# Graph layers on one Trainium2 core: the first group's loads moved ahead of the weights, bias rows made from broadcast loads

## Chip, cores and metric

The kernel runs on one core of a Trainium2 chip. The metric is the device time of one execution in microseconds. The engines are named as in the profile: PE is TensorE (PEld its weight loads), DVE is VectorE, ACT is ScalarE, POOL is GpSimd, SP is SyncE, whose queue issues every DMA of this kernel.

## What is computed

There are 128 graphs of 128 nodes with 64 features, and a dense adjacency matrix of each, with zeros. Two layers follow one another, each with a residual sum and a normalisation:

```python
x = layernorm(x + L0(x, adj));  x = layernorm(x + L1(x, adj))

def L0(x, adj, W1, b1, W2, b2):            # 64 -> 192 -> 64
    mask = adj > 0;  W1a, W1b = W1[:64], W1[64:]
    h = relu((x @ W1a)[:, :, None, :] + (x[:, :, None, :] - x[:, None, :, :]) @ W1b + b1)
    hm = einsum('bjkh,bjk->bjh', h, mask)
    return hm @ W2 + mask.sum(-1)[..., None] * b2

def L1(h, A, W1, b1, W2, b2, W_ih, b_ih, W_hh, b_hh):
    m = relu(relu(h @ W1 + b1) @ W2 + b2)
    msg = relu(A @ m)
    i_r, i_z, i_n = split(msg @ W_ih.T + b_ih);  h_r, h_z, h_n = split(h @ W_hh.T + b_hh)
    r, z = sigmoid(i_r + h_r), sigmoid(i_z + h_z)
    return (1 - z) * tanh(i_n + r * h_n) + z * h
```

## The kernel before

The 128 graphs are worked in 32 groups of four (`G`). The hard part is layer 0's sum over neighbours of a relu of a sum. The kernel writes `h` as a node's part plus a neighbour's part, gathers the neighbours' parts and sums absolute values. For each group:

- `load`: SP issues four transfers, `adjT` (256 KB), `xT` in two halves, `x`.
- `masks` (POOL) makes `maskT` from `adjT`; `ranks` (PE `pc`, then VectorE `rankT`) numbers each node's neighbours; `degrees` and `counts` (`nseg`, `wseg`, `npad`) and `offsets` (`side`, `past`, `own`, `own32`) say which overflow rows belong to which node; `turned` and `places` lead to `place`.
- `picks` makes one-hot selection matrices from `rankT` (`pick0`) and `place` (`pick1`).
- `values0` and `values1`: PE multiplies `xT` with `wall`, the joined weights of layer 0, and adds a bias with `call3`; ScalarE copies the result to `uv`.
- `pieces` splits a part of `uv` into three bf16 numbers `b0`, `b1`, `b2` that add up to it: a ScalarE cast, a VectorE subtraction, a ScalarE cast, a POOL subtraction.
- `seed` (ScalarE writes the node's part to PSUM), `gather` (twelve PE matmuls of `pick` and `b`, line 592, add the neighbours' parts) and `reduce` (VectorE sums absolute values, line 608) come 24 times per group. This is the main loop.
- `together` and `sums` collect the results, `second` to `update` finish layer 0 and compute layer 1 (`gw1`, `gw2`, `gb1`, `gb2`, `wm`, `wx`, `bias3`).

The order on each engine is written out by hand. `TIMETABLE` gives each part a list of times; a part is a Python generator, and each time runs it up to its next `yield`. Group g is shifted by 768 (`PER`). All steps of all groups are sorted by time and recorded in that order, so each engine's instructions, SP's DMAs too, stand in the order of the timetable. An engine does not overtake a waiting instruction. Group 1's `load` is due before much of group 0's work, and group 1's `masks`, `ranks` and `degrees` are recorded ahead of group 0's first gather.

Everything of the setup is recorded ahead of the plan, lines 95 to 225: constants (`ident`, `upper`, `incl`, `strict`, `iota`), weights, and bias rows. PE adds a bias by a matmul of ones with a bf16 matrix that holds, in rows 0 to 2 (and again 64 to 66), three bf16 pieces of the bias that add up to it. The helper `three_rows` makes it from one row: on one partition it casts and subtracts, and each piece goes to its rows by DMA, as many as halves and repetitions ask (6 for `call3`, 12 for `gb2`, 12 for `bias3`). `wall` is computed on 64 partitions and copied to the other 64 by a DMA (line 192). PSUM tiles of the small products come from a pool `ps_w` with two buffers, so a product waits for the reading of the last but one.

The path at the end of the kernel (a loop over graphs behind a flag, for graphs with too many neighbours) has the same helpers.

Of the kernel before, what the change touches and what calls it, by code (L numbers as in the profile page):

```python
# [8 lines left out]
F32 = mybir.dt.float32  # L9
BF16 = mybir.dt.bfloat16  # L10
I32 = mybir.dt.int32
AF = mybir.ActivationFunctionType
ALU = mybir.AluOpType
AX = mybir.AxisListType

N = 128
F = 64
H = 192
HC = 96
G = 4  # L20
K = 64
V = H + F
W0 = 8
W1 = 4
# [25 lines left out]


# [17 lines left out]
def adj_resnorm_kernel(  # L69
# [19 lines left out]
    nc = tc.nc  # L89
# [6 lines left out]
    make_identity(nc, ident)  # L96
    ident_h = const.tile([N, N], BF16, name="ident_h")
    nc.vector.tensor_copy(ident_h, ident)
    upper = const.tile([N, N], F32, name="upper")
    make_upper_triangular(nc, upper)  # L100

    incl = const.tile([N, N], BF16, name="incl")
    nc.vector.tensor_copy(incl, upper)
    incl2 = const.tile([N, N], BF16, name="incl2")
    nc.vector.tensor_copy(incl2, upper)
    nc.vector.memset(incl2[0:K, K:N], 0.0)

    halves = const.tile([N, 2], BF16, name="halves")
    nc.vector.memset(halves, 0.0)
    for h in range(2):  # L110
        nc.vector.memset(halves[h * K : (h + 1) * K, h : h + 1], 1.0)
    strict = const.tile([N, N], BF16, name="strict")
    nc.vector.tensor_sub(strict, upper, ident)
    strict_w = const.tile([N, N], BF16, name="strict_w")
    nc.vector.tensor_scalar_mul(strict_w, strict, -float(W1))
    ones_h = const.tile([N, N], BF16, name="ones_h")
    nc.vector.memset(ones_h, 1.0)
    ones = const.tile([1, N], F32, name="ones")
    nc.vector.memset(ones, 1.0)
    nhalf = const.tile([N, G], F32, name="nhalf")  # L120
    nc.gpsimd.memset(nhalf, -0.5)
    nseg_all = const.tile([N, NB], BF16, name="nseg_all")

    wb = const.tile([F, H], F32, name="wb")
    nc.sync.dma_start(wb, w1[F : 2 * F, :])
    wa = const.tile([F, H], F32, name="wa")
    nc.sync.dma_start(wa, w1[0:F, :])
    iota = const.tile([N, N], BF16, name="iota")

    wall = const.tile([N, 4 * N], F32, name="wall")  # L130
    nc.vector.tensor_add(wall[0:F, 0:H], wa, wb)
    nc.vector.tensor_scalar_mul(wall[0:F, V : V + H], wb, -1.0)
    w2c = const.tile([HC, 2, F], F32, name="w2c")
    for c in range(2):
        nc.sync.dma_start(w2c[:, c, :], w2[c * HC : (c + 1) * HC, :])
    nc.vector.tensor_scalar_mul(w2c, w2c, 0.5)

    def row(name, src, n):
        t = const.tile([1, n], F32, name=name)
        nc.sync.dma_start(t, src.rearrange("(o n) -> o n", o=1))  # L140
        return t

    def three_rows(name, src, n, times, halves=2):

        t = const.tile([N, times, n], BF16, name=name)
        nc.vector.memset(t, 0.0)
        rest = src
        for c in range(3):
            piece = const.tile([1, n], BF16, name=f"{name}_piece{c}")
            nc.vector.tensor_copy(piece, rest)  # L150
            for at in (c, F + c)[:halves]:
                for i in range(times):
                    nc.sync.dma_start(t[at : at + 1, i, :], piece)
            if c < 2:
                left = const.tile([1, n], F32, name=f"{name}_left{c}")
                nc.vector.tensor_sub(left, rest, piece)
                rest = left
        return t


    call = const.tile([1, V], F32, name="call")
    nc.sync.dma_start(call[:, 0:H], b1.rearrange("(o h) -> o h", o=1))
    b2row = row("b2row", b2, F)
    b2bc = const.tile([N, F], F32, name="b2bc")
    wT = const.tile([HC, 4, F], F32, name="wT")
    b1c = const.tile([HC, 2], F32, name="b1c")
    for c in range(2):
        nc.sync.dma_start(b1c[:, c : c + 1], b1[c * HC : (c + 1) * HC].rearrange("(h o) -> h o", o=1))
    with tc.tile_pool(name="ps_c", bufs=1, space=bass.MemoryType.PSUM) as ps_c:
        ips = ps_c.tile([N, N], F32, name="ips")  # L170
        nc.tensor.matmul(ips, ones_h, strict, start=True, stop=True)
        nc.vector.tensor_copy(iota, ips)
        b2ps = ps_c.tile([N, F], F32, name="b2ps")
        nc.tensor.matmul(b2ps, ones, b2row, start=True, stop=True)
        nc.vector.tensor_copy(b2bc, b2ps)

        tps = ps_c.tile([HC, 4, F], F32, name="tps")
        for c in range(4):
            at = (V, V + HC, 0, HC)[c]
            nc.tensor.transpose(tps[:, c, :], wall[0:F, at : at + HC], ident[0:F, 0:F])  # L180
        nc.vector.tensor_copy(wT, tps)
        dps = ps_c.tile([F, 2, F], F32, name="dps")
        for d in range(2):
            for c in range(2):
                nc.tensor.matmul(dps[:, d, :], wT[:, 2 * d + c, :], w2c[:, c, :], start=c == 0, stop=c == 1)
        nc.vector.tensor_copy(wall[0:F, H:V], dps[:, 0, :])
        nc.vector.tensor_copy(wall[0:F, V + H : 4 * N], dps[:, 1, :])
        cps = ps_c.tile([1, F], F32, name="cps")
        for c in range(2):
            nc.tensor.matmul(cps, b1c[:, c : c + 1], w2c[:, c, :], start=c == 0, stop=c == 1)  # L190
        nc.vector.tensor_add(call[:, H:V], cps, b2row)
    nc.sync.dma_start(wall[F:N, :], wall[0:F, :])
    call3 = three_rows("call3", call, V, 1)

    def twice(name, src):
        t = const.tile([N, N], F32, name=name)
        nc.vector.memset(t, 0.0)
        for h in range(2):  # L200
            nc.sync.dma_start(t[h * F : (h + 1) * F, h * F : (h + 1) * F], src)
        return t

    gw1 = twice("gw1", g_w1)
    gw2 = twice("gw2", g_w2)
    gb1 = const.tile([N, 1], F32, name="gb1")
    for h in range(2):
        nc.sync.dma_start(gb1[h * F : (h + 1) * F], g_b1.rearrange("(h o) -> h o", o=1))
    gb2 = three_rows("gb2", row("gb2row", g_b2, F), F, G, 1)


    wm = const.tile([N, H], F32, name="wm")
    wx = const.tile([N, H], F32, name="wx")
    for h in range(2):
        hs = slice(h * F, (h + 1) * F)
        nc.sync.dma_start(wm[hs, 0:F], w_ihT[:, 128:H])
        nc.sync.dma_start(wm[hs, F:H], w_ihT[:, 0:128])
        nc.sync.dma_start(wx[hs, :], w_hhT)
    bi = row("bi", b_ih, H)
    bh = row("bh", b_hh, H)  # L220
    bcat = const.tile([1, 256], F32, name="bcat")
    nc.vector.tensor_copy(bcat[:, 0:F], bi[:, 128:H])
    nc.vector.tensor_add(bcat[:, F:H], bi[:, 0:128], bh[:, 0:128])
    nc.vector.tensor_copy(bcat[:, H:256], bh[:, 128:H])
    bias3 = three_rows("bias3", bcat, 256, 2)
# [13 lines left out]
    def tail_parts(s, work, ps_w, n, store):  # L239


        name = s["name"]
# [47 lines left out]
        def message2():  # L290
            p = ps_w.tile([N, n, F], F32, tag="w", name=f"pn{name}")
            nc.tensor.matmul(p, ones_h, gb2, start=True, stop=False)
            for i in range(2):
                nc.tensor.matmul(p[:, 2 * i : 2 * i + 2, :], s["m1"][:, i, :], gw2, start=False, stop=i == 1)
            yield
            s["m2"] = work.tile([N, n, F], F32, tag="m2", name=f"m2_{name}")
            nc.scalar.activation(s["m2"], p, AF.Relu)
# [13 lines left out]
        def gates():  # L311
# [3 lines left out]
            for h in range(2):  # L315
                nc.tensor.matmul(ps[h], ones_h[hs[h]], bias3[hs[h]], start=True, stop=False)
# [42 lines left out]
    with ExitStack() as fast:  # L359
# [6 lines left out]


        zeros = loads.tile([N, 512], BF16, name="zeros", bufs=1)
        nc.vector.memset(zeros, 0.0)
        for i in range(3):  # L370
            p = ps_g.tile([N, 2, 512], F32, tag="g", name="pv")
            for c in range(2):
                nc.tensor.matmul(p[:, c, :], ones_h, zeros, start=True, stop=True)
# [13 lines left out]
        def prep_parts(s):  # L387
            g = s["g"]
# [116 lines left out]
            def values(i):  # L505
                def part():
# [4 lines left out]
                    for h in range(2):  # L511
                        ks = slice(h * F, (h + 1) * F)
                        nc.tensor.matmul(ps[h][:, 0:V], ones_h[ks], call3[ks, 0, :], start=False, stop=True)  # L513
# [8 lines left out]
            def pieces():  # L522

                v = s["uv"][:, :, H : V + H]

                def piece(c):
                    s[f"b{c}"] = prep.tile([N, G, H + F], BF16, tag=f"b{c}", name=f"b{c}_{g}")
                    return s[f"b{c}"]

                nc.scalar.copy(piece(0), v)  # L530
                yield
                r = prep.tile([N, G, H + F], F32, tag="r", name=f"r{g}", bufs=1)
                nc.vector.tensor_sub(r, v, s["b0"])  # L533
                yield
                nc.scalar.copy(piece(1), r)  # L535
                yield
                nc.gpsimd.tensor_tensor(piece(2), r, s["b1"], ALU.subtract)  # L537
# [146 lines left out]
        plan = {}  # L684
        for g in range(ng):
# [7 lines left out]
            for name, times in TIMETABLE.items():  # L693
                run = parts[name]()
                for t in times:
                    plan.setdefault(g * PER + t, []).append(run)
# [127 lines left out]
```

## Time and profile before

| | us |
|---|---|
| median of 3 runs (lowest, highest) | 1123.66 (1123.61, 1123.87) |
| time of the profiled execution | 1123.7 |
| its span | 1121.9 |
| VectorE busy | 1046.6 |
| PE busy | 989.1 |
| ScalarE busy | 929.2 |
| POOL busy | 790.0 |
| group 0's `adjT` issued | 25.48 |
| first reduction of line 608 | 50.23 |

The span runs from the first to the last instruction of the profile; busy times are sums of instruction times, and instructions of one engine may overlap a little. In the profile's lines `a<-b` says that `a` is made from `b`. The bracket at the end of a timeline line is the idle time of the engine before it and what released it. SPq is SP's queue, with the time it takes to issue a DMA.

### The profile page before, as it was taken

Reading aid. Unit: us, or ns where it says so; the run is one execution under the profiler, and the core shown is the slowest. Engines: PE = TensorE matmul, PEld = TensorE weight load, DVE = VectorE, ACT = ScalarE, POOL = GpSimd, SP = SyncE. Lnnn points to the kernel's source line nnn. Section 1 sums busy time; section 2 is a strip of 40 time slices with the busy share of each in tenths; the row PEclk is TensorE's granted clock in tenths of the full one; section 3 lists DMA queues with packets and bytes.
Section 4 is the critical chain, followed back from the end, with each engine's and each line's share of the span. In section 5 each row is a group of like instructions: output and inputs, shape, how many; then the busy total and the mean of one; then the engine's idle time right before and its main releaser. Section 6 shows DMA issues by size and latency. Waiting matters only on the chain.

```text
span 1121.9 us, 33471 instructions
## 1 busy us (share of the span) xinstructions
PE 989.1 (88%) x13434; PEld 767.5 (68%) x13434; DVE 1046.6 (93%) x2446; ACT 929.2 (83%) x1570; POOL 790.0 (70%) x1161
## 2 busy tenths in 40 slices
PE   2689999999999999999999999999999999999872
PEld 1457777777777777777777776777777677777761
DVE  3599999999999999999999999999999999999961
ACT  0489988988888898888989888898888889888850
POOL 0365667777867877787777778777777877787656
PEclk9999999999999999999999999999999999999985
DMA  1200000000000000000000000000000000000000
GB/s 32 64 1 21 21 21 10 13 25 25 25 26 25 14 14 25 26 25 25 26 20 7 25 25 26 25 26 25 2 25 25 26 25 25 26 7 2 7 6 26
DMA packets 21722, 23.73 MB, mean 21 GB/s; under 512 B 4727, under 2 KB 17402, under 8 KB 21562
## 3 DMA queue, kind: packets, MB, share of 16 engines
q1 hardware_dynamic: 21562, 21.54, 6.4%
q8 instruction: 107, 1.75, 0.6%
q14 instruction: 53, 0.43, 0.1%
HBM read 17.19 MB, written 4.19 MB: 19 GB/s over the span
## 4 chain that ended last, share of the span: by engine, by line
DVE 46%; PE 29%; ACT 15%; issue 5%; POOL 3%; SPq 1%; DMA 0%; DVEq 0%; ACTq 0%; POOLq 0%
DVE part L608 29%; PE pv L592 11%; ACT pv L561 10%; PE pw L267 6%; DVE pick L500 4%; PE pu L510 4%; PE ph L650 3%; ACT uv L517 3%; DVE r L533 3%; PE ph L649 2%; DVE rankT L401 2%; DVE n L331 2%; DVE stats L248 1%; DVE own L450 1%; DVE rh L330 1%
## 5 line engine op out<-in xcount | busy, mean ns | idle before, releaser
L608 DVE TENSOR_REDUCE part<-pv 128x192 f32<-128x768 f32 x768 | 697.3, 944 | 10.8 <-PE pv L592 7.0
L592 PE MATMUL pv<-b,pick 64*128 64x192 bf16 x9216 | 509.9, 244 | 55.6 <-ACT pv L561 49.3
L592 PEld LDWEIGHTS <-pick 64*128 64x128 bf16 x9216 | 379.7, 94 | 166.2 <-issue 135.4
L561 ACT COPY pv<-uv 128x768 f32<-128x768 f32 x512 | 404.1, 807 | 30.8 <-DVE part L608 30.4
L630 POOL TENSOR_TENSOR part<-part 128x384 f32<-128x384 f32 x128 | 132.6, 1036 | 235.7 <-DVE part L608 235.5
L561 ACT COPY pv<-us 128x768 f32<-128x768 f32 x256 | 206.7, 808 | 28.9 <-DVE part L608 23.7
L650 PE MATMUL ph<-ownT,part 128*96 128x128 f32 x512 | 95.6, 282 | 23.0 <-POOL part L637 22.9
L650 PEld LDWEIGHTS ph<-ownT,part 128*96 128x96 f32 x512 | 70.4, 167 | 35.5 <-POOL part L637 35.5
L517 ACT COPY uv<-pu 128x512 f32<-128x512 f32 x128 | 68.5, 586 | 23.4 <-PE pu L513 21.2
L500 DVE TENSOR_SCALAR pick<-rankT 128x512 bf16<-128x512 bf16 x256 | 86.5, 349 | 0.0
L510 PE MATMUL pu<-wall,xT 64*128 64x512 f32 x256 | 82.0, 645 | 0.0
L267 PE MATMUL pw<-w2c,hmT 96*128 96x64 f32 x512 | 79.9, 289 | 0.0
L632 POOL TENSOR_TENSOR part<-part 128x192 f32<-128x192 f32 x128 | 75.9, 593 | 5.2
L634 POOL TENSOR_TENSOR part<-part 128x192 f32<-128x192 f32 x128 | 74.3, 591 | 5.0
L637 POOL TENSOR_TENSOR part<-part 128x192 f32<-128x192 f32 x128 | 75.1, 597 | 1.4 <-DVE part L608 1.4
L649 PE MATMUL ph<-ident,part 128*96 128x128 f32 x256 | 73.1, 286 | 2.7 <-POOL part L634 1.8
L267 PEld LDWEIGHTS pw<-w2c,hmT 96*128 96x128 f32 x512 | 68.7, 195 | 9.8 <-issue 5.0
L255 POOL TENSOR_TENSOR rs<-ve,nhalf 128x4 f32<-128x4 f32 x64 | 67.0, 1047 | 5.3
L537 POOL TENSOR_TENSOR b<-r,b 128x1024 bf16<-128x1024 f32 x32 | 68.2, 2130 | 0.5 <-ACT b L535 0.5
L392 POOL TENSOR_SCALAR maskT<-adjT 128x512 bf16<-128x512 f32 x32 | 49.7, 1554 | 26.6 <-DMA adjT<-in_adjT_dram 26.6
L656 ACT COPY hmT<-ph 96x512 f32<-96x512 f32 x64 | 36.6, 572 | 33.5 <-PE ph L650 33.5
L572 PE MATMUL pz<-uv,own 128*128 128x192 f32 x256 | 62.5, 368 | 0.9 <-ACT uv L517 0.5
(150 smaller groups left out, 1638.5 us busy)
## 6 DMA issues: line engine op xcount, KB each, us to landing
adjT<-in_adjT_dram SPq DMA_DIRECT2D x32, 256.0 KB, 2.7
xT<-in_xT_dram SPq DMA_DIRECT2D x64, 64.0 KB, 2.5
x<-in_x_dram SPq DMA_DIRECT2D x32, 128.0 KB, 2.3
out_dram<-o SPq DMA_DIRECT2D x32, 128.0 KB, 2.0
gb<-gb_piece SPq DMA_DIRECT2D x12, 0.1 KB, 1.6
bias<-bias_piece SPq DMA_DIRECT2D x12, 0.5 KB, 1.7
wall<-wall SPq DMA_DIRECT2D x1, 128.0 KB
call<-call_piece SPq DMA_DIRECT2D x6, 0.5 KB, 1.7
```

The source lines that it names most:

```text
L267: nc.tensor.matmul(p[:, i, :], s["hmT"][:, i, c, :], w2c[:, c, :], start=c == 0, stop=False)
L500: nc.vector.tensor_scalar(s[name][:, i], s[src], float(first + i), None, ALU.is_equal)
L510: nc.tensor.matmul(ps[h], s["xT"][ks, i, :], wall[ks, :], start=True, stop=False)
L517: nc.scalar.copy(uv[:, 2 * h + i, :], ps[h])
L561: nc.scalar.copy(v, src.rearrange("p (c b h) -> p c b h", c=1, b=1).to_broadcast(list(v.shape)))
L592: nc.tensor.matmul(v[:, h, j, :], pick[ks, a + j, i, :], s[f"b{c}"][ks, i, F : F + H], start=False, stop=c == 2, skip_group_check=True,)
L608: nc.vector.tensor_reduce(into, view(s["pv", i, k]).rearrange("p c b h -> p h c b"), AX.XY, ALU.add, apply_absolute_value=True,)
L630: nc.gpsimd.tensor_tensor(f[:, 0:2], f[:, 0:2], f[:, 2:4], ALU.add)
L632: nc.gpsimd.tensor_tensor(f[:, 0], f[:, 0], f[:, 1], ALU.add)
L637: nc.gpsimd.tensor_tensor(f[:, 0], f[:, 0], f[:, 1], ALU.add)
L649: nc.tensor.transpose(p[:, i, c, :], s["part", i0 + i][:, 0, cs], ident)
L650: nc.tensor.matmul(p[:, i, c, :], s["part1", i0 + i][:, 0, cs], s["ownT"][:, i0 + i, :], start=False, stop=True, skip_group_check=True,)
```

## The change

The setup becomes a generator that the plan runs at five times (`SETUP`), and group 0 has its own times (`FIRST`), so both are recorded together in one order:

- Group 0's `load` (-5000) comes first of all on SP. Then the setup's first step issues `wab` (both halves of layer 0's first weights on each half of the partitions, two transfers), `w2c`, `b1c`, and five biases. Each bias is loaded to all 128 partitions by a source that repeats the row. The other weights (`gw1`, `gw2`, `gb1`, `wm`, `wx`) are the setup's last step, at -3000: after all of group 0's preparation in the record, and ahead of group 1's `load` (-752). `gw1` and `gw2` are cleared by VectorE in that step, ahead of their transfers.
- The bias matrix is computed on all partitions for all 576 columns at once: three casts, two subtractions, and a product or multiply-add of each piece with a column of `at`, which is one in the rows where that piece belongs. It needs no DMA. The matmuls that repeat a bias read it with a repeating pattern (`each`). `gb2` now has its rows twice, and is halved before.
- `wall` is computed on all 128 partitions, so its copy is gone; `wT` is written twice over for that.
- Constants are recorded in the order of their use; the small products share `ps_w`.
- For group 0 `pieces` runs graph by graph, four passes over 256 columns; the other groups have one pass over 1024 columns as before.

```diff
+SETUP = (-4990, -4988, -4987, -4981, -3000)
+FIRST = {
+    "load": (-5000,), "masks": (-4989,), "ranks": (-4986, -4985), "degrees": (-4984, -4983), "counts": (-4982,),
+    "offsets": (-4980, -4979, -4966, -4965, -4964, -4963, -4962, -4962), "turned": (-4978, -4977),
+    "values0": (-4976, -4975, -4974), "values1": (-4971, -4970, -4969), "pieces": (-4972, -4968, -4959, -4958),
+    "places": (-4961, -4960), "pick0": (-4973, -4973, -4967, -4967, -4957, -4957, -4956, -4956),
 }
...
-    def three_rows(name, src, n, times, halves=2):
...
-    nc.sync.dma_start(wall[F:N, :], wall[0:F, :])
-    call3 = three_rows("call3", call, V, 1)
...
-    gb2 = three_rows("gb2", row("gb2row", g_b2, F), F, G, 1)
...
-    bias3 = three_rows("bias3", bcat, 256, 2)
...
+    call3, bias3, gb2 = three[:, 0:V], three[:, V : V + 256], three[:, V + 256 : NBI]
...
+    def each(t, n):
+        return t.rearrange("p (o c) -> p o c", o=1).to_broadcast([t.shape[0], n, t.shape[1]])
+
+    def setup(ps_g, ps_w):
+        def spread(t, src):
+            nc.sync.dma_start(t, src.rearrange("(o n) -> o n", o=1).to_broadcast(list(t.shape)))
+        for h in range(2):
+            nc.sync.dma_start(wab[h * F : (h + 1) * F], w1.rearrange("(c f) h -> f c h", c=2))
+        nc.sync.dma_start(w2c, w2.rearrange("(c h) f -> h c f", c=2))
+        nc.sync.dma_start(b1c, b1.rearrange("(c h) -> h c", c=2))
+        spread(b2bc, b2)
+        spread(bias[:, 0:H], b1)
+        spread(bi, b_ih)
+        spread(bias[:, V + F : V + 256], b_hh)
+        spread(bias[:, V + 256 : NBI], g_b2)
...
+        yield
+        nc.vector.tensor_copy(iota, ips)
+        nc.vector.tensor_add(wall[:, 0:H], wab[:, 0, :], wab[:, 1, :])
+        nc.vector.tensor_scalar_mul(wall[:, V : V + H], wab[:, 1, :], -1.0)
...
+        yield
...
+        nc.vector.tensor_copy(wT, tps.rearrange("p c (o f) -> p c o f", o=1).to_broadcast([HC, 4, 2, F]))
+        yield
...
+        nc.vector.tensor_copy(wall[:, H:V], dps[:, 0, :])
+        nc.vector.tensor_copy(wall[:, V + H : 4 * N], dps[:, 1, :])
+        nc.vector.tensor_add(bias[:, H:V], cps, b2bc)
...
+        nc.vector.tensor_add(at, ident[:, 0:3], ident[:, F : F + 3])
+        piece = const.tile([N, NBI], BF16, name="piece")
+        for c in range(3):
+            nc.vector.tensor_copy(piece, bias)
+            if c == 0:
+                nc.vector.tensor_scalar(three, piece, at[:, c : c + 1], None, ALU.mult)
+            else:
+                nc.vector.scalar_tensor_tensor(
+                    out=three, in0=piece, scalar=at[:, c : c + 1], in1=three, op0=ALU.mult, op1=ALU.add
+                )
+            if c < 2:
+                nc.vector.tensor_sub(bias, bias, piece)
+        yield
+        for t, src in ((gw1, g_w1), (gw2, g_w2)):
+            nc.vector.memset(t, 0.0)
+            for h in range(2):
+                nc.sync.dma_start(t[h * F : (h + 1) * F, h * F : (h + 1) * F], src)
+        for h in range(2):
+            hs = slice(h * F, (h + 1) * F)
+            nc.sync.dma_start(gb1[hs], g_b1.rearrange("(h o) -> h o", o=1))
+            nc.sync.dma_start(wm[hs, 0:F], w_ihT[:, 128:H])
+            nc.sync.dma_start(wm[hs, F:H], w_ihT[:, 0:128])
+            nc.sync.dma_start(wx[hs, :], w_hhT)
...
-            nc.tensor.matmul(p, ones_h, gb2, start=True, stop=False)
+            nc.tensor.matmul(p, ones_h, each(gb2, n), start=True, stop=False)
...
+                for gs in [slice(i, i + 1) for i in range(G)] if g == 0 else [slice(0, G)]:
+                    v = s["uv"][:, gs, H : V + H]
+                    nc.scalar.copy(b[0][:, gs], v)
...
+                    nc.vector.tensor_tensor(r[:, gs], v, b[0][:, gs], ALU.subtract)
...
+                    nc.scalar.copy(b[1][:, gs], r[:, gs])
...
+                    nc.gpsimd.tensor_tensor(b[2][:, gs], r[:, gs], b[1][:, gs], ALU.subtract)
+                    yield
...
+        name, g, run = "setup", -1, setup(ps_g, ps_w)
+        for t in SETUP:
+            plan.setdefault(t, []).append(run)
...
-                for t in times:
+                for t in FIRST.get(name, times) if g == 0 else times:
```

## Prediction

> **What bounds the kernel now.** I read the page first, then the windows over the start, then the timeline and the chain of waits there. The page gives the whole: VectorE 93% busy, and its largest group, the reduction on line 608, waits 10.8 us in 1122.
>
> ```profile
> PE 989.1 (88%) x13434; PEld 767.5 (68%) x13434; DVE 1046.6 (93%) x2446; ACT 929.2 (83%) x1570; POOL 790.0 (70%) x1161
> L608 DVE TENSOR_REDUCE part<-pv 128x192 f32<-128x768 f32 x768 | 697.3, 944 | 10.8 <-PE pv L592 7.0
> ```
>
> So from the first reduction on VectorE is the bound, and time can come only from the start or from less VectorE work later. The windows show where the start ends (columns: length, then busy us of PE, PEld, DVE, ACT, POOL):
>
> ```profile
> 0.00:20.00 20.00, 6.11 (x25) 3.08 (x26) 7.00 (x36) 1.28 (x1) 1.12 (x9) 1.00 0.10 18
> 20.00:40.00 20.00, 7.54 (x31) 4.06 (x31) 8.82 (x33) 2.41 (x5) 4.50 (x8) 1.00 0.28 77
> 40.00:60.00 20.00, 13.90 (x118) 9.46 (x117) 11.29 (x27) 12.38 (x21) 7.14 (x11) 0.91 0.13 39
> 60.00:80.00 20.00, 15.64 (x233) 11.33 (x228) 19.43 (x30) 16.84 (x26) 11.17 (x16) 1.00 0.01 2
> ```
>
> VectorE is idle for over half of the first 60 us. The timeline of that stretch (start, length, instruction, idle before and releaser) says why:
>
> ```profile
> 4.64 2.39 SPq L201 DMA_DIRECT2D gw<-in_g_w_dram  x4
> 7.08 1.23 SPq L208 DMA_DIRECT2D gb<-in_g_b_dram  x2
> 13.99 7.49 SPq L153 DMA_DIRECT2D gb<-gb_piece  x12
> 22.15 0.59 SPq L218 DMA_DIRECT2D wx<-in_w_hhT_dram  x1
> 25.48 0.36 SPq L379 DMA_DIRECT2D adjT<-in_adjT_dram  x1
> 28.32 1.50 POOL L392 TENSOR_SCALAR maskT<-adjT 128x512 bf16<-128x512 f32 x1 [26.61 <-DMA adjT<-in_adjT_dram]
> 33.33 0.66 DVE L443 TENSOR_SCALAR side<-iota,off 128x128 bf16<-128x128 bf16 x1
> 50.23 1.92 DVE L608 TENSOR_REDUCE part<-pv 128x192 f32<-128x768 f32 x2 [4.06 <-PE pv L592]
> ```
>
> The SP queue spends 0.2 to 0.6 us on an issue whatever its size, mostly 0.62. Group 0's adjacency is asked for only at 25.48, after 42 small transfers; its mask starts at 28.32. The first reduction runs at 50.23. The chain of waits just before that:
>
> ```profile
> 41.40 1.65 PE pz L572 x4
> 43.05 0.44 PE pc L398
> 43.51 0.69 DVE rankT L401
> 44.71 1.31 POOL rnd L418
> 47.16 2.09 POOL b L537
> 49.30 0.84 PE pv L592 x8
> 50.23 0.91 DVE part L608
> ```
>
> On every engine group 1's ranks (`pc` and `rankT`) stand ahead of group 0's first gather. In the changed program's order this is still so, and from the first reduction on all engines have the same instructions in the same order as before. So the question is one number: when does the first reduction start? 1071.7 us (1121.9 - 50.23) follow it either way.
>
> **What the change removes and adds.** Gone are 30 row copies on SP (6 call, 12 gb, 12 bias; 18.6 us of issue at 0.62), `wall`'s copy, and five single-row loads. Added are five broadcast loads, one VectorE chain over 576 columns, and four quarter-size passes of `pieces` for group 0 instead of one. adjT is now issued at 0.73; by the 2.84 us from 25.48 to 28.32 its mask starts at 3.6 and ends at 5.1. That is not what sets the start any more. The weights come after it.
>
> Step 1, when the bias rows (`three`) are ready. The second `wab` transfer is issued after 0.36 + 1.11 + 0.59 + 0.62 us and gaps, at 3.5. `wx` landed 2.1 us after issue, so it lands at about 5.7. The trace shows no such two-row load, nor a partition broadcast: the nearest rows, `x` with 128 rows (2.3 to landing) and `gb2row` (1.36), bound the landing from both sides; for the issue I take 0.62, and 0.2 to 1.2 as ends (the 0.22 of b2row, two patterns' worth). The five broadcasts are issued by 8.3 and land by 10.4.
> Then, in order: wall's two halves (0.35 + 0.25) to 6.35; four transposes 0.70; `wT`, 96x512 from PSUM, 0.68 (the 96x256 row took 0.41, 1.04 ns per further column), to 7.8. `rankT` now stands here on VectorE: 0.69, and 0.2 for deg and larger, to 8.7. cps and dps on PE behind them (0.75 + 1.15), to 10.45. Nine small VectorE operations of 0.06 to 0.28, to 11.65. The chain over 576 columns: casts took 0.182 at 64 columns and 0.28 at 256, so 0.445 at 576; subtractions 0.212 and 0.412, so 0.745; the two multiply-adds 0.81 (0.281 at 64 columns, same slope); the product 0.29. With 0.03 between, three casts, two subtractions, one product, two multiply-adds make 4.95. `three` is ready at 16.6.
>
> Step 2, from there to the gw memset. The memsets of `gw1` and `gw2` now stand at the 50th and 51st place of VectorE, behind all of group 0's preparation. In order: bias matmul 0.47; uv copy 0.58; values1 at PE's slow early rate 2.8 (37.97 to 40.76; line 510 takes about 1.15 a matmul until 59 us, 0.645 on the whole run's mean); two copies 1.07; a quarter cast on ScalarE 0.37 (x1T's 128x256 row); a quarter subtraction 0.45; two picks 0.42; side and past 1.3 (eight at 0.16, as at 58.79); own 0.46; place's matmuls 0.98 (37.00 to 37.97); place 0.62; then cast, subtraction, cast, cast, subtraction 2.1; four picks 0.85; memset 0.2. With gaps 12.75. POOL's quarter pieces, 0.55 each (2.13 for the whole), now run beside VectorE's picks.
> [...] The row at 33.33 above is a 0.25 us instruction that took 0.66 beside POOL's mask; the eight took 2.0 instead of 1.3, so 1.5 us of POOL cost 0.7. [...] by the row half, and the first of them finds VectorE waiting anyway. I take 0.35. Step 2 is 13.1, and the memset done at 29.7[...].
>
> Step 3, what is queued behind that memset. SP waits for it before the gw transfers, and behind them stand gb1, wm, wx and **group 1's loads**. Twelve issues at 0.62 (4.64 to 8.31 for six of them): 7.5. So group 1's adjT is issued at 37.2, against 27.68 before: it becomes 9.5 us later, while all of group 0 becomes earlier. Mask start 40.05, end 41.6; pc 0.62, rankT 0.7, the second pz 1.7, twelve gather matmuls at the slow rate 1.2 (1.15 for the twelve at 56.66). First reduction at 45.95, against 50.23: 4.3 us earlier. b2's 2.09, on the chain before, is off it, done by about 30. The second reduction finds twelve slow matmuls (1.15) instead of a finished set: 0.15 back. Counts of group 1 come about 1 us earlier only, but had 4.7 us of slack (nseg at 46.3, used at 51.01). Later weights (gw, wx) are needed first at 94.8 us (gw, line 285). In the main loop operands change only their addresses: nothing.
>
> [...]
>
> **Sum.** 4.3 - 0.15 = 4.1. The profiled execution took 1123.7 with a span of 1121.9; its time equals the median of 1123.66. Prediction: span 1117.8, time **1119.6**.
>
> **Rivals.** Break-even is a memset done at 34.0: from there group 1's late load costs more than group 0's early one brings.
> (a) Slower: the broadcasts. If each of the nine setup loads ahead of the bias chain takes 1.2 us to issue instead of 0.62 (no row shows one), `three` comes 5 to 6 us later, the memset at 35, and group 1's wait gives about 1125. For it: four-byte and repeated rows are new shapes. Against: 64x1 columns (gb1) took 0.62 like all else. 7%.
> (b) Given back: group 1, whose preparation comes only 1 us earlier while its turn comes 4 earlier, stalls between 50 and 70; or PE stays slow longer. Gain 0.5 to 2, about 1122.3. Against: the slack named above. 13%.
> (c) More: the chains of Steps 1 and 2 are shorter ([...]the memset at 27.5): gain 6.3, 1117.4. 18%.
> (d) It does nothing because another path sets the first reduction: excluded by the order, since adjT 0 and all b pieces are earlier; under 2%.
> The main case has 60%, 1118.2 to 1121.1.
>
> About 0.2% (2.2 us) is what a measurement of this kernel can tell from no change. Faster by more: main, (c) and a little of (b), 0.82. Same: most of (b), 0.11. Slower 0.07. The range leaves out the end of (a) and the far end of (c): 1116.6 to 1122.7.
>
> **What would show it.** adjT 0's mask at 3.6; `three` finished at 16 to 18; the gw memset near 30 with SP idle from about 8.5 until then; group 1's adjT at 37; POOL's second mask released by that DMA and not by POOL; first reduction at 46; then the same windows as before, 4 us earlier. Wrong if the first reduction is later than 49, or if VectorE between 50 and 80 us is idle longer than before.

## Result and profile after

| | before | after |
|---|---|---|
| median of 20 runs each (lowest to highest), us | 1123.37 (1121.09 to 1124.59) | 1121.46 (1119.38 to 1123.41) |
| profiled execution, us; its span | 1123.7; 1121.9 | 1119.77; 1118.0 |
| first reduction of line 608 | 50.23 | 49.14 |
| group 1's `adjT` issued | 27.68 | 40.24 |

The changed kernel is faster by a little, ratio 0.9985 (95% interval 0.9978 to 0.9992): 1.9 us, about half of the 4.1 forecast. The profiled execution's span of 1118.0 looks like the forecast's 1117.8, but that is luck: it is the third fastest of the twenty, and the row below the span says that the first reduction came 1.1 us earlier and not 4.3.

The page of the changed kernel, its totals and the reduction's group: VectorE's busy time (1046.6 before) is almost unchanged, so nothing after the start was made cheaper for it.

```profile
PE 987.4 (88%) x13432; PEld 766.5 (69%) x13432; DVE 1045.6 (94%) x2438; ACT 930.0 (83%) x1576; POOL 789.6 (71%) x1164
L608 DVE TENSOR_REDUCE part<-pv 128x192 f32<-128x768 f32 x768 | 696.6, 943 | 9.0 <-PE pv L592 4.8
```

The windows of the changed kernel over the same stretch (length, busy us of PE, PEld, DVE, ACT, POOL, granted clock, DMA share, GB/s):

```profile
0.00:20.00 20.00, 10.23 (x40) 5.67 (x40) 10.03 (x36) 2.03 (x3) 3.96 (x16) 0.70 0.20 57
20.00:40.00 20.00, 6.15 (x21) 3.50 (x20) 7.15 (x27) 7.38 (x16) 2.90 (x4) 0.50 0.04 9
40.00:60.00 20.00, 12.42 (x127) 8.97 (x128) 10.59 (x27) 8.85 (x16) 5.49 (x11) 0.60 0.29 84
60.00:80.00 20.00, 15.85 (x232) 11.52 (x228) 20.00 (x31) 16.75 (x25) 12.28 (x17) 1.00 0.01 2
```

Work came forward into the first 20 us (VectorE 10.03 against 7.00), but VectorE is busy for only 7.15 of the next 20, and the DMA share of that window fell from 0.28 to 0.04: SP stands still there. The granted clock of 0.50 is no new slowness: four `pz` passes take 1.65 as they did before (41.40 there); the column shows 1.00 until the trace's first clock record, which comes at 52.8 us in the kernel before and at 4.7 in the changed one. The timeline of the changed kernel names the waits:

```profile
7.44 0.43 SPq L148 DMA_DIRECT2D bias<-in_g_b_dram  x1
13.48 0.19 DVE L203 COPY bias<-bi 128x64 f32<-128x64 f32 x1 [1.34 <-DMA bi<-in_b_ih_dram]
14.66 0.20 DVE L206 TENSOR_SCALAR bias<-bias 128x64 f32<-128x64 f32 x1 [0.56 <-DMA bias<-in_g_b_dram]
14.89 0.46 DVE L211 CAST piece<-bias 128x576 bf16<-128x576 f32 x1
18.97 0.82 DVE L215 SCALAR_TENSOR_TENSOR three<-piece,at,three 128x576 bf16<-128x576 bf16 x1
32.48 0.30 DVE L223 MEMSET gw<- 128x128 f32 x2
32.68 2.41 SPq L225 DMA_DIRECT2D gw<-in_g_w_dram  x4
40.24 0.58 SPq L377 DMA_DIRECT2D adjT<-in_adjT_dram  x1
```

The bias loads, issued by 7.9, are waited for until 14.66; `three` is finished at 19.8, the memsets follow at 32.5, SP starts again at 32.68 and reaches group 1's `adjT` at 40.24. The chain of waits from there:

```profile
40.24 3.07 DMA adjT<-in_adjT_dram
43.39 1.50 POOL maskT L390
44.93 0.60 PE pc L396
45.56 0.70 DVE rankT L399
46.30 1.65 PE pz L572 x4
47.95 1.09 PE pv L592 x12
49.14 0.91 DVE part L608
```

It is a different chain from that of before: group 1's transfer is now at its head, and group 0's `b2` is no longer on it.

### The profile page after: what moved, and what is told of

Its sections match the earlier page's. It is cut to its first block, busy times and chain, and to the rows that moved or that the text cites. A ratio compares the mean times of both kernels' runs of the same rounds, so it can differ in the third digit from the quotient of the medians.

```text
span 1118.0 us, 33420 instructions
## 1 busy us (share of the span) xinstructions
PE 987.4 (88%) x13432; PEld 766.5 (69%) x13432; DVE 1045.6 (94%) x2438; ACT 930.0 (83%) x1576; POOL 789.6 (71%) x1164
## 4 chain that ended last, share of the span: by engine, by line
DVE 46%; PE 29%; ACT 16%; issue 5%; POOL 2%; SPq 1%; DMA 1%; DVEq 0%; ACTq 0%; POOLq 0%
DVE part L608 29%; PE pv L592 11%; ACT pv L561 10%; PE pw L273 6%; DVE pick L498 4%; PE pu L508 3%; PE ph L650 3%; DVE r L530 3%; ACT uv L515 3%; PE ph L649 2%; DVE n L337 2%; DVE rankT L399 2%; DVE stats L254 1%; DVE own L448 1%; DVE rh L336 1%
## 5 line engine op out<-in xcount | busy, mean ns | idle before, releaser
L536 POOL TENSOR_TENSOR b<-r,b 128x1024 bf16<-128x1024 f32 (+1 forms) x35 | 69.0, 1970 | 20.0 <-ACT b L533 20.0
```

## Experiments

In these sections "first" is the start of the first reduction of line 608. Its distance to 50.23 is the more exact measure of what happened in the start, as long as the next reductions follow it at the same distance (they do not in e5); total times of single runs scatter, the twenty of the changed kernel over 4 us.

| run | edit to the changed kernel, unless said | first | us |
|---|---|---|---|
| e4_distinct_rows | bias loads read 128 different rows | 46.72 | 1119.99 |
| e1_load1_first | other weights after group 1's load | 38.99 | 1111.45 |
| e2_clear_early | `gw` cleared at the start | 38.53 | 1109.37 |
| e5, e5b_loads_only | kernel before, two loads first | 31.48, 31.74 | 1107.08, 1110.09 |
| e6_loads_last | all weights first, then loads | 49.47 | 1121.64 |
| e7_mask1_early | e1, group 1's load and mask earlier | 38.73 | 1109.18 |
| e3_whole_pieces | e1, `pieces` whole | 37.64 | 1109.56 |
| e8_old_order | e1, group 0 in its old times | 36.95 | 1110.52 |
| e10_split | e8, bias chain in two parts | 32.32 | 1105.64 |
| e11_warm | e10, PE kept busy ahead of `values0` | 31.24 | 1104.3 |

Ratios to the kernel before, from four runs each with 95% intervals: e1 0.9894 (0.9878 to 0.9911), e5b 0.9879 (0.9863 to 0.9896), e10 0.9843 (0.9827 to 0.986), e11 0.9822 (0.9806 to 0.9838). The other times are of one run.

**What made the bias rows late.** The host hands over one more input, `rows`, in which the five biases are laid out 128 times; the bytes loaded are the same.

```diff
-            nc.sync.dma_start(t, src.rearrange("(o n) -> o n", o=1).to_broadcast(list(t.shape)))
+            nc.sync.dma_start(t, src)
...
-        spread(bi, b_ih)
+        spread(bi, rows[:, V : V + H])
```

> The changed kernel, but the five bias loads read 128 copies of the row laid side by side in memory by the host (each partition its own copy) in place of the same row 128 times. Theory: the broadcasts land 5.7 to 7 us after their issue because all partitions read the same few bytes; with copies of their own they land 2 to 3 us after issue, the bias chain starts near 12.0 instead of 14.7, and everything up to the memset, group 1's load and the first reduction comes about 2.6 us earlier (46.5). Rival: they are late because they queue behind the 700 KB of the loads ahead; then landing and first reduction stay where they are (49.1).

The DMA view, issues by size and median us from issue to landing, first of the changed kernel, then of this one:

```profile
b2bc<-in_b_dram SPq DMA_DIRECT2D x1, 32.0 KB, 4.3
bi<-in_b_ih_dram SPq DMA_DIRECT2D x1, 96.0 KB, 7.0
bias<-in_g_b_dram SPq DMA_DIRECT2D x1, 32.0 KB, 7.2
```

```profile
bi<-in_rows_dram SPq DMA_DIRECT2D x1, 96.0 KB, 2.0
bias<-in_rows_dram SPq DMA_DIRECT2D x1, 32.0 KB, 2.0
```

The timeline of this kernel has no wait on a bias any more, and the chain starts as soon as the matmuls of `dps` are read:

```profile
11.55 0.22 DVE L201 COPY wall<-dps 128x64 f32<-128x64 f32 x1 [2.77 <-PE dps L200]
12.48 0.46 DVE L212 CAST piece<-bias 128x576 bf16<-128x576 f32 x1
46.72 1.92 DVE L609 TENSOR_REDUCE part<-pv 128x192 f32<-128x768 f32 x2 [2.33 <-PE pv L593]
```

Reading one row for all partitions cost up to 5 us of landing, 2.41 of them on the path (14.89 against 12.48), and the first reduction moved by 2.42. The size is not it, since the same bytes from 128 rows landed in 2.0. The five loads land one behind another (at 9.8, 11.7, 13.5, 13.8 and 14.6, issue plus landing), so the last one's 7.2 seems to hold a wait for those ahead of it. The total of this one run, 1119.99, lies within the scatter of the changed kernel.

**What made group 1 late.** First the setup's last step is put behind group 1's load, then, in another kernel, only the two memsets are moved to VectorE's first constants.

```diff
-SETUP = (-4990, -4988, -4987, -4981, -3000)
+SETUP = (-4990, -4988, -4987, -4981, -700)
```

> The changed kernel with one time altered: the setup's last step (clearing of gw1 and gw2, and the twelve weight transfers) is recorded after group 1's load and not ahead of it. Theory: the first reduction (49.1 us in the changed kernel's profile) waits for group 1's load, which stands on SP behind the clearing of gw1 (32.5 us) and twelve issues (7.5 us). Then here adjT of group 1 is issued near 8 us; its mask can start as soon as POOL is through with group 0's pieces (33.1 us) instead of at 43.4, and the first reduction comes at about 38.9; the time falls by 10 us against the changed kernel, 12 against the kernel before, to about 1111. Rival: group 0's own chain (bias rows, pieces, place) sets the first reduction and the load only looks like the releaser: then it stays at 48 to 49 and the time within 1 us of the changed kernel.

```diff
+        nc.vector.memset(gw1, 0.0)
+        nc.vector.memset(gw2, 0.0)
...
-            nc.vector.memset(t, 0.0)
```

> The changed kernel, with the two memsets of gw1 and gw2 among VectorE's first constants; the twelve weight transfers stay ahead of group 1's load. Theory: what delays group 1's load is the wait on the memset, not the number of transfers. SP then issues the twelve without a pause from 8 to 16 us, adjT of group 1 lands near 19, long before POOL is free at 33.1; first reduction at 38.9 as if the load stood first. Rival: the twelve issues themselves are the price: then the gain is at most the pause, and the first reduction comes no earlier than about 45.

The timelines, group 1's load, its mask and the first reduction, e1 and then e2:

```profile
7.92 0.43 SPq L377 DMA_DIRECT2D adjT<-in_adjT_dram  x1
33.11 1.62 POOL L390 TENSOR_SCALAR maskT<-adjT 128x512 bf16<-128x512 f32 x1
38.99 1.92 DVE L608 TENSOR_REDUCE part<-pv 128x192 f32<-128x768 f32 x2 [2.32 <-PE pv L592]
```

```profile
7.98 2.40 SPq L226 DMA_DIRECT2D gw<-in_g_w_dram  x4
17.66 0.58 SPq L378 DMA_DIRECT2D adjT<-in_adjT_dram  x1
32.65 1.62 POOL L391 TENSOR_SCALAR maskT<-adjT 128x512 bf16<-128x512 f32 x1
38.53 1.92 DVE L609 TENSOR_REDUCE part<-pv 128x192 f32<-128x768 f32 x2 [2.33 <-PE pv L593]
```

Both come out as expected. In e2 all twelve transfers still stand ahead of group 1's load on SP, and the result is the same as with none: what held group 1 was SP's wait for the memset, not the number of transfers. The mask no longer waits for a DMA (no bracket) but stands behind group 0's `pieces` on POOL, so the 10 us by which e1 loads it earlier bring nothing over e2.

**The loads alone.** The kernel before, with nothing but the transfers of groups 0 and 1 put first on SP:

```diff
+    for st in states[0:2]:
+        load(st)
...
-                load(s)
+                if s["g"] > 1:
+                    load(s)
```

> The kernel before, with only the loads of groups 0 and 1 issued ahead of all other transfers; bias rows are still made on one partition and spread by 30 copies, constants and parts in the order of before. Theory: the load of group 0 at the end of SP's queue was what kept the kernel before back; call3 and wall are complete near 17 to 19 us, values0 follows, and from there the 17.5 us of the kernel before (32.7 to 50.2) lead to a first reduction near 37. Rival: the row copies hold SP and with it the bias that values0 needs, so the first reduction comes at 44 or later and the load's place alone brings less than half.

> Again the kernel before with nothing but the transfers of groups 0 and 1 ahead of the weights, now in rounds against the kernel before. The one look gave the first reduction at 31.48 and 1107.1 us. Theory (this single move is the whole gain, and the rest of the change costs more than it brings): 1106 to 1108.5, ratio 0.985 to 0.987, and within 2.5 us of the kernel with the split bias chain on the same chip. Rival (the one look was a lucky phase of the granted clock): 1109 or more.

The first reduction came at 31.48, 5.5 earlier than expected and 7.5 ahead of e1. Part of it is PE: the six zero matmuls that clear PSUM stand in the middle of `values0` here and end at 17.3, and behind them a pass of line 514 takes 0.59 (at 18.01), where two ahead of them took 2.07 (from 12.60); in e5b the four passes of `pz` at 25.75 take 0.92, those at 44.26 in the kernel before 1.65. But the ratio is that of e1 (the intervals overlap), and the rival of the second expectation has it: e5's 1107.08 was at the lower end, and the second set has a median of 1110.09. The trace shows VectorE waiting again inside group 0 (the third reduction starts 3.8 after the first, against 2.6 in the kernel before), which gives back 1.2 us of the early start; where the rest went is not shown. So the old way of making the biases, with 30 row copies, is not slower than e1 as a whole.

**The opposite end.** All weights first, with `gw` cleared at the start, then the loads, with everything else of the change:

```diff
-    "load": (-5000,), ...
+    "load": (-4989.5,), ...
```

> The changed kernel with the transfers in the place of the kernel before: all weights first (gw1 and gw2 cleared among the first constants), then the loads of groups 0 and 1. What is left of the change is the bias rows from broadcasts, the own times of group 0 and the order of constants. Theory: without the wait on the memset even this beats the changed kernel. adjT of group 0 is issued near 14 us, its mask ends near 18; pc stands ahead of cps and dps on PE, so the bias matrix is ready near 26.5; from there the 19.1 us seen in e1_load1_first (19.9 to 39.0) give a first reduction near 45.5. Rival: the early place of group 0's load is what the change lives on; then the first reduction is at 50 us or later, no better than before.

A miss: first at 49.47 instead of 45.5, close to the rival's 50. Without the early load the rest of the change is worth 0.8 us here. From `three` to the reduction took 19.1 as expected, but `three` was late (30.4 for 26.5). Group 0's mask ended at 20.25 and not at 18, and SP's own rows show why:

```profile
8.28 0.56 SPq L165 DMA_DIRECT2D gb<-in_g_b_dram  x1
10.86 0.47 SPq L166 DMA_DIRECT2D wm<-in_w_ihT_dram  x1
11.37 0.60 SPq L167 DMA_DIRECT2D wm<-in_w_ihT_dram  x1
12.60 0.47 SPq L168 DMA_DIRECT2D wx<-in_w_hhT_dram  x1
15.67 0.58 SPq L377 DMA_DIRECT2D adjT<-in_adjT_dram  x1
```

The issues behind the bias loads stop for 2.0 us (8.84 to 10.86) and again for 0.6. In e2 they stop for 1.2 and 1.3 us between 10.38 and 13.32, while VectorE waits for the last bias row until 14.29. What SP waited for in these gaps is not shown. The other 1.6 us lie between the mask and `three`, 10.1 where 8.5 was put.

**The order of group 0.** Three kernels ask what binds once group 1's load is early. Group 1's load and mask pulled ahead of group 0's `pieces`:

```diff
+SECOND = {"load": (-4989.8 - PER,), "masks": (-4981.5 - PER,)}
...
```

> e1_load1_first, with group 1's load and its mask further ahead in the record: the mask stands on POOL behind group 0's counts, not behind group 0's four quarter pieces. Theory: in e1_load1_first the first reduction (39.0 us) waited for POOL to be through with the pieces and then the mask; here pc of group 1 can run at 30 us, and what ends last is group 0's own: the copy us on ScalarE at 32, two seeds, twelve gather matmuls; first reduction at 34.5 to 35.5. Rival: the matmuls pz and the bias rows set it in any case, and it stays at 38 to 39.

```profile
16.48 1.63 POOL L391 TENSOR_SCALAR maskT<-adjT 128x512 bf16<-128x512 f32 x1 [5.46 <-DMA adjT<-in_adjT_dram]
32.53 0.69 DVE L531 TENSOR_TENSOR r<-uv,b 128x256 f32<-128x256 f32 x1 [0.78 <-ACT b L528]
35.16 0.68 DVE L400 TENSOR_TENSOR rankT<-pc,maskT 128x512 bf16<-128x512 f32 x1
```

The expected 4 us did not come. The mask is done at 18, but group 1's `rankT` on VectorE is recorded behind the last quarter of `pieces` (32.53), picks and memsets, and it has no bracket: it waited for nothing but its turn. From `three` to the first reduction took 17.4 against e1's 19.1, but group 0 itself came 1.4 later (`three` at 21.3 for 19.9): the last bias row was waited for until 15.67 and not 14.77, and a subtraction of the chain took 1.16 instead of 0.75 beside POOL's early mask. With whole `pieces` in the change's order (and four times of their own for it in `FIRST`):

```diff
-                for gs in [slice(i, i + 1) for i in range(G)] if g == 0 else [slice(0, G)]:
+                for gs in [slice(0, G)]:
...
```

> The changed kernel with group 1's load issued first (first reduction at 38.99, time 1111.4), and beside that group 0's pieces as one pass of 1024 columns on each engine as in the kernel before, instead of four passes of 256. Theory: in group 0 the passes for graphs 2 and 3 stand behind place and the picks on VectorE; with one pass ahead of them the wait of one engine for the other goes, and of the 3.6 us which the old order of group 0 as a whole was worth, about 2.8 come from this edit: first reduction at 36.2, time about 1108.7. Rival: the pieces are not what counts in that order (the place of the bias step is): first reduction within 0.5 of 39.0 and time within 1 of 1111.4.

First at 37.64: 1.35 earlier than e1, half of the theory's 2.8, so neither side has it whole. A row that may hold the other half stands on VectorE: a `past`, elsewhere 0.24, took as long as POOL's whole piece beside it, and `own`, the matmuls of `place` and `pz` come behind it.

```profile
27.86 2.19 DVE L442 TENSOR_SCALAR past<-iota,off 128x128 bf16<-128x128 bf16 x1
27.88 2.12 POOL L533 TENSOR_TENSOR b<-r,b 128x1024 bf16<-128x1024 f32 x1 [16.92 <-ACT b L531]
```

And with group 0's old times (whole `pieces`, the bias step at -140, and group 1's load as early as in e7):

```diff
-SETUP = (-4990, -4988, -4987, -4981, -3000)
-FIRST = {"load": (-5000,), "masks": (-4989,), ... }
+SETUP = (-4990, -4988, -4987, -140, -130)
+FIRST = {"load": (-5000,)}
```

> Broadcast bias rows as in the changed kernel and the loads of groups 0 and 1 first, but group 0's parts in the times of the kernel before (pieces in one pass of 1024 columns); the bias chain is recorded just ahead of values0, the weights behind it. Theory: the order that the change gives group 0 costs time: the pieces of graphs 2 and 3 stand behind place on ScalarE, so b2 is complete only 13.2 us after the bias rows. In e5_loads_only, with the order of before, the first reduction came 13.5 us after the bias (17.9 to 31.5), against 19.1 in e1_load1_first; with the bias matrix ready near 19.7 here the first reduction comes at 33 to 34. Rival: the bias rows' lateness is all that matters and the order is neutral; then it comes at 38 to 39 as in e1_load1_first.

First at 36.95, later than the expected 33 to 34: `three` came at 21.4 instead of 19.7, and from there it took 15.5 us instead of 13.5. But against e1's 19.1 this is less: the new order of group 0 costs 3.6 us; whole `pieces` alone gave back 1.1 of it, counted from `three` in the same way (18.0).

**A better version.** In e8 the chain over 576 columns is cut: the 256 columns that `values0` needs first, the other 320 behind group 0's `own`.

```diff
+        split(slice(0, V))
+        yield
...
+        split(slice(V, NBI))
```

> e8_old_order with the bias chain in two parts: the 256 columns that values0 needs first, the other 320 columns (layer 1's) behind group 0's own. Theory: the chain of 576 columns and its wait for the last broadcasts (14.7 us) hold values0; with b1 and b2 alone it can start near 12.5 and takes 3 us, the bias is ready near 15.5 and the first reduction comes at 29 to 30, 2 us ahead of e5_loads_only; the time falls to about 1105, 18 below the kernel before. Rival: PE in its slow state or the rest of the chain on VectorE takes it back: first reduction at 31.5 or later and no gain on e5_loads_only.

Then the six zero matmuls go from the start of the program to just ahead of `values0`.

```diff
+        for i in range(3):
+            p = ps_g.tile([N, 2, 512], F32, tag="g", name="pv")
+            for c in range(2):
+                nc.tensor.matmul(p[:, c, :], ones_h, zeros, start=True, stop=True)
```

> The kernel with the bias chain split and group 0 in the old order, with one move: the six matmuls of zeros that clear the pv tiles stand just ahead of the matmuls of values0, after those of dps, instead of at the start of the program. The name 'dps' ends at 13.2 us in the run before; the six take 0.45 each or a little more and are done near 16, while VectorE makes the bias rows of the call part (ready at 16.8). Theory (PE is slow there because it stood idle before): values0 and values1 take 0.4 to 1.1 us for each pass as they did where the loads alone were moved, group 0's pz takes about 1 us instead of 1.65, and the first reduction comes at about 30.0 instead of 32.3: time about 1103.3. Rival (the slow passes come from something else, such as the operands or the share of granted clock): the six only delay values0 by 0 to 2.7 us and the first reduction stays at 32.3 or comes as late as 34: time 1105.6 to 1107.

The timelines of e10 and then of e11:

```profile
13.67 2.20 PE L510 MATMUL pu<-wall,xT 64*128 64x512 f32 x4 [0.45 <-DMA bi<-in_b_ih_dram]
19.98 2.81 PE L510 MATMUL pu<-wall,xT 64*128 64x512 f32 x4
23.48 1.65 PE L571 MATMUL pz<-uv,own 128*128 128x192 f32 x4 [0.47 <-ACT uv L517]
32.32 1.92 DVE L607 TENSOR_REDUCE part<-pv 128x192 f32<-128x768 f32 x2 [4.07 <-PE pv L591]
```

```profile
15.87 1.15 PE L510 MATMUL pu<-wall,xT 64*128 64x512 f32 x4
22.30 1.08 PE L571 MATMUL pz<-uv,own 128*128 128x192 f32 x4 [0.57 <-ACT uv L517]
28.13 2.12 POOL L535 TENSOR_TENSOR b<-r,b 128x1024 bf16<-128x1024 f32 x1
31.24 1.92 DVE L607 TENSOR_REDUCE part<-pv 128x192 f32<-128x768 f32 x2 [4.60 <-PE pv L591]
```

In e10 the bias rows of `values0` are ready at 16.8, but PE is slow, with 2.20 and 2.81 for the two times four passes of line 510 and 1.65 for `pz`: the first reduction came at 32.32 and not at 29 to 30, as the rival said. It is 0.6 later than in e5b, yet the third reduction (34.95 against 35.55) and the total time are ahead. In e11 the first passes take about half the time and the first reduction comes at 31.24. So the operands are not what made them slow: the same matmuls took 1.15 with 2.8 us of zero matmuls right ahead of them and 2.20 without. Idling alone is not it either, since in e10 2.8 us of `cps` and `dps` end 0.45 ahead of the slow passes. What decides it is not shown: where the six matmuls stand at the start of the program, the four passes of `tps` 1 to 3 us later take 0.40 in four of the traces (the changed kernel, e1, e4, e8) and 0.63 in the other five (e2, e3, e6, e7, e10).

Only 1.1 of the 2.3 us came, and in total time the intervals of e10 and e11 overlap. As far as the rows show, three things took the rest: the bias rows came 0.4 later (17.2); the granted clock was 0.81 in 20 to 30 and 0.68 in 30 to 40, and twelve gather matmuls took 1.14 at 32.17, against 0.67 at 37.38 in e5b; and POOL's `b2`, for which the gathers wait, starts 0.8 after its input is ready, behind group 1's counts on POOL (0.3 in the kernel before). e11 is the best version found, faster than e5b on the same chip (the intervals do not overlap).

## Why the prediction was half right

The mechanism, its order and its path were right: adjT 0's mask started at 3.7 (3.6 forecast); SP stood idle until the memset; POOL's second mask was released by its DMA. The size was not. The time of 1121.46 lies in the stated range, but outside the main case (1118.2 to 1121.1), and the gain of 1.9 is under the 2.2 from which it called a change measurable, a case to which it gave 0.11. That the range held it is in part luck. By its own sign the prediction was wrong: "if the first reduction is later than 49", and it came at 49.14. The three steps against the trace of the changed kernel:

| | forecast | measured |
|---|---|---|
| Step 1: chain over 576 columns starts | 11.65 | 14.89 |
| its length | 4.95 | 4.9 |
| `three` ready | 16.6 | 19.8 |
| Step 2: from `three` to SP's restart | 13.1 | 12.9 |
| Step 3: twelve issues | 7.5 | 7.56 |
| mask 1 starts after the issue | 2.85 | 3.15 |
| from there to the first reduction | 5.9 | 5.75 |
| first reduction | 45.95 | 49.14 |

- **Step 1 is the step that failed**, and all of the 3.2 us lie in the start of its chain. The term "the five broadcasts are issued by 8.3 and land by 10.4" was mis-sized. They were issued by 7.9, at 0.43 to 0.45 each and not 0.62, and the last one was waited for until 14.66, where 10.4 was forecast. I had bounded the landing by `x` and `gb2row` from both sides; neither row reads one source 128 times, so they did not bound it. e4 prices this at 2.4 us. The other 0.8 is mostly `cps` and `dps`, put at 0.75 and 1.15 and measured 1.11 and 1.91: e4, without the wait, starts the chain at 12.48 and not at 11.65.
- **Step 2 came out right as a sum** (12.9). One of its terms did not: what POOL's pieces cost VectorE was put at 0.35 us, an estimate from the row of before at 33.33. Beside POOL's pieces of 0.75 and 0.67 a `side` took 0.67 instead of 0.25 (the row below) and a subtraction 0.69 instead of 0.42: 0.7 together, and other terms came out lower. The first of the three pieces found VectorE waiting, and the other two were met part way. In e3, where one piece of 2.12 met VectorE at work, a `past` took 2.19. The row at 33.33 is beside POOL's mask and not beside a piece.

```profile
25.96 0.67 DVE L441 TENSOR_SCALAR side<-iota,off 128x128 bf16<-128x128 bf16 x1
```

- **The chain's length**: the rows' 4.95 met the 4.9: the casts took 0.46 each, the product 0.37 (0.29 forecast), the subtractions 0.75, the multiply-adds 0.82.
- **Step 3 was right**; e2 shows that SP's wait was the cause, and e1 its price: 10 us.
- **Break-even** was put at a memset done at 34.0. It was done at 32.8, and the gain was 1.1, which fits.
- **Rival (a)** had the right place and the wrong price: it was not the issue but the landing. **Rival (b)** has the size of the gain (0.5 to 2) but not its cause: from 50 to 80 us VectorE is idle for 1.5 us, against 1.7 before, and from 60 on never.
- **The sum.** The start gave 1.1 where 4.1 was forecast (the 0.15 for the second reduction did not come: it starts 0.96 after the first in both). The profiled execution is 3.9 shorter, since its tail was shorter too. In the timeline of before and then after, the last reduction and layer 0's result:

```profile
1083.99 0.96 DVE L608 TENSOR_REDUCE part<-pv 128x192 f32<-128x768 f32 x1 [0.40 <-PE pv L592]
1092.46 0.42 DVE L272 TENSOR_TENSOR y<-pw,t 128x256 f32<-128x256 f32 x1 [7.51 <-PE pw L665]
```

```profile
1081.74 0.96 DVE L608 TENSOR_REDUCE part<-pv 128x192 f32<-128x768 f32 x1 [0.40 <-PE pv L592]
1088.47 0.42 DVE L278 TENSOR_TENSOR y<-pw,t 128x256 f32<-128x256 f32 x1 [5.77 <-PE pw L665]
```

The wait for `pw` is 7.51 in one and 5.77 in the other for the same instructions. The granted clock falls to 0.5 at 1087.1 before and at 1086.7 after (from 1084 to 1088 its mean is 0.89 and 0.84), but the changed kernel's last reduction is 2.2 earlier, so more of those matmuls run at the full clock: in its trace four passes of `pw` take 0.64 ahead of the fall and 1.10 behind it. Another 0.8 comes near 316 us, whose cause I did not find, and 0.3 in small steps. The median's gain of 1.9 lies between the start's 1.1 and the profile's 3.9; that the rest of it is this phase of the clock is argued, since the other executions have no trace.

## What to carry to other kernels

A load that is moved or added is worth its landing, not its issue (4.3 to 7.2 us against 0.43 to 0.45 for the bias loads here): look for a row of the same access pattern (one source row for all partitions is its own case), and where there is none, take a wide range. When an instruction on a queue waits for another engine, list what stands behind it: here one small clear of a tile, placed late on VectorE, held the next group's input for 25 us and ate nearly all that the change had won (e1 and e2 get 10 us more by moving one step or the clears alone). After this start had been shortened, the next bound was the order in which the engines' instructions were recorded (3.6 us between e1 and e8); read a row without a bracket as "it waited for its turn".

## What the runs showed of the hardware

- Five loads of one DRAM row to all 128 partitions, one behind another, landed 4.3 to 7.2 us after their issue in the changed kernel, with 128 different rows of the same size 1.8 to 2.1 us (e4). Behind such loads the next issues of the same queue stopped for 2.0 and 0.6 us (e6) and for 1.2 and 1.3 us (e2).
- SP took 0.43 to 0.45 us for an issue of these loads, with one row as with 128 different ones, and 0.59 for most others (the changed kernel and e4).
- SP issued nothing from 7.9 to 32.68 us in the changed kernel, where the transfer at its turn waited for a memset that started at 32.48. In e1, where group 1's load stands ahead of that transfer, the load was issued at 7.92.
- VectorE and POOL: beside POOL's piece of 2.12 us a VectorE instruction that elsewhere took 0.24 took 2.19 (e3); beside POOL's mask of 1.49 one of 0.25 took 0.66, the next two 0.24 each, and the three after them 0.38 to 0.64 (the kernel before, from 33.33).
- PE at the start: four 64-row float32 passes took 2.2 to 2.8 us in e10 and 1.15 in e11, right after 2.8 us more of back-to-back matmuls. The clock column does not tell the two apart: it shows 1.00 from 13 to 20 us in both.
- In the tail the granted clock fell to 0.5 at 1087.1 us before and 1086.7 after; in the changed kernel four passes of `pw` took 0.64 ahead of it and 1.10 behind it. The wait for `pw` was 7.51 us before and 5.77 after, where the last reduction stood 2.2 us earlier.
